# A conv-attention network's first pair: ones products on TensorE, a convolution shared by four engines, work made ahead; squares on ScalarE in layer 1; the last product in pieces

## The chip, the cores and the metric

The kernel runs on one core of one Trainium2 chip. The metric is device time in microseconds (us); lower is better. Times before are from three runs. Engines are named as in the profile: PE is TensorE, DVE is VectorE, ACT is ScalarE, POOL is GpSimd; SP only issues transfers here.

## What is computed

The input x is (2, 512, 32, 32) in float32; four layers follow one another. All arithmetic is float32.

```
layer 0: xn = bn(x);  q = grouped 1x1 conv of xn (8 groups of 64 channels)
         off = tanh(pw @ gelu(depthwise conv 6x6, stride 4, of q)) * 4      # 8x8 points per group
         kv  = bilinear samples of xn at the 64 shifted points;  k, v = grouped 1x1 convs of kv
         pos = query grid - shifted points;  bias = sign(pos) * log1p(|pos|)
         bias = w3 @ relu(w2 @ relu(w1 @ bias + b1) + b2) + b3               # 128 wide, 1024 x 64 positions
         x  += out_w @ softmax(q k / 8 + bias) v;   x += mlp(bn(x))
layer 1: linear attention: q, k of 64 channels brought to unit length, x += gamma * (v sums) / (n + q . sum k)
layer 2, 3: group norm, 8-head attention over 1024 positions, projection, residual
```

The bias network in layer 0 is evaluated for 2 x 8 groups, 64 sample points and 1024 queries; its second layer (w2) is the largest part of the kernel.

## The kernel before

**Layer 0** works through eight pairs of groups (a pair is 128 channels, pairs[0] to pairs[7]) and, for each group u, 16 steps of four sample points (`quads`: u, o, jj). For a step, `first_hidden` has DVE make the first hidden layer h1 (L528, four instructions of 1024 columns, each the sum of a row table x and a column table y, clipped at zero); `second_hidden` multiplies it on PE (L559, four q blocks of eight products; every product is two instructions), ScalarE takes the relu out of PSUM (L564), and ScalarE, GpSimd and adding transfers join the four blocks (flips of sign by ScalarE, L566 and L570, or by GpSimd, L568 and L575, both 128x1024). `last_product` adds into the logits, `attend` does the softmax. Two generators run behind this stream, one step at a time: `offsets` (from xn to the offsets and the logs of a pair) and `sampled` (samples, keys and values).

For pair 0, all of `offsets` runs before the stream begins. In it: xn (L295) on DVE, the padded query image qpad from products L308 and copies L317, the 36 taps of the strided convolution (for pair 0, 18 by ScalarE, L326, and 18 by DVE, L335, then two reductions over taps, L352), Gelu, the pw product (L368), Tanh, and from it the log of positions. Between steps 4 and 5 DVE prepares the last weights (`last_weights`, `fold_weights`). The tables x and y of pair 0's first points are made by masks (L492) and a product with a tile of ones, `self.all` (L499), read by L508 and L509. `sampled` transposes xn on PE (L413) and copies it by ScalarE (L414).

The order on PE, ACT, DVE and POOL is the order of the program text (`manual_schedule`); each engine takes its instructions in that order. PSUM holds a pool of three tiles of two banks (`ps`, shared by hp, transposes, tables and queries), one bank `self.bank` and one for the logits. Transfers are queued on SP (x, logs, results), on ACT (weights, at the start) and on POOL (the adding ones).

**Layer 1** has the order: products of queries and keys (L897) with additions on DVE (L900) for the two images and halves, squares on GpSimd (L908) after the second half of each image, `unit_length(0)` (L912 to L918), then 16 blocks of transposes (L927), copied to xT in turn by ACT and DVE (L930). The transposes use two PSUM pools of three tiles in turn; the products L897 use the second of them too. The products of keys with xT (L958) come later; they have 128x128 weights and 65 columns. Within the part whose order is written out GpSimd is not included.

**The end.** Layer 3's projection is seven products of half-size blocks per image (`project`); the last, P4, fills a PSUM tile with two blocks (p = 0, 1), then DVE adds each to x (L1489) and SP sends it out (L1497).

Of the kernel before, what the change touches and what calls it, by code (L numbers as in the profile page):

```python
# [18 lines left out]
P = 128  # L19
# [35 lines left out]
class Net:  # L55
# [16 lines left out]
    def prologue(self, ctx: ExitStack):  # L72
# [4 lines left out]
        nc.scalar.dma_start(self.cols, io["cols"])  # L77
# [21 lines left out]
    def layer0(self):  # L99
# [3 lines left out]
        with ExitStack() as ctx:  # L103
            keep = self.pool(ctx, "l0")
            self.l0qkv = keep.tile([P, 3, CT, P], F32, tag="qkv", name="qkv")
            nc.scalar.dma_start(self.l0qkv[:, 0], io["l0_qkv"][:, 0])
# [6 lines left out]
            last_weights = self.last_weights(keep)  # L113
            next(last_weights)
            nc.scalar.dma_start(self.l0qkv[:, 1:3], io["l0_qkv"][:, 1:3])
            ow = keep.tile([P, CT, C], F32, tag="ow", name="ow")
# [23 lines left out]
            with self.tc.manual_schedule(engines=engines):  # L140
                pairs = [{} for _ in range(BP)]
                for n, _ in enumerate(self.offsets(pairs[0], 0, ps)):
                    if n == 4:
                        nc.vector.tensor_copy(self.ys, self.grid[:, G_Y : G_Y + NB])
                        next(last_weights, None)
                        self.fold_weights()
                front = [self.sampled(pairs[0], 0, ps)]
                after, sims, att = [], {}, None
                tables = {}
                quads = [(u, o, jj) for u in range(2 * BP) for o in range(8) for jj in range(2)]  # L150
                ready = self.first_hidden(*quads[0], pairs, tables)
                held, self.join = [], None
                for i, (u, o, jj) in enumerate(quads):
# [12 lines left out]
                    else:  # L166
                        first = z
                        if len(held) == 2:
                            v, last, zs = held.pop(0)
                            self.last_product(v, last, zs, sims, ps_s)  # L170
                            if last == 7:
                                if v % 8 == 0:
                                    self.advance(after, lambda: False)
                                    att = [
                                        apool.tile([P, N], F32, tag=f"att{t}", name=f"att{v}_{t}") for t in range(CT)
                                    ]
# [44 lines left out]
    def last_weights(self, keep):  # L221
# [16 lines left out]
        nc.vector.tensor_tensor(self.flip, sign[:, 0:3], sign[:, 3:4].to_broadcast([P, 3]), ALU.mult)  # L238
        self.ends = keep.tile([P, 60], F32, tag="ends", name="ends")
        nc.vector.memset(self.ends, 0.0)  # L240
        for k in range(4):
            rows = slice(32 * k, 32 * k + 32)
            nc.vector.tensor_copy(self.ends[rows, 28 + k : 29 + k], sign[rows, 3:4])

# [43 lines left out]
    def offsets(self, m, bt, ps):  # L288
# [5 lines left out]
        xn = m["xn"] = self.fone.tile([P, N], F32, tag="xn", name=f"xn{b}{t}")  # L294
        nc.vector.tensor_scalar(xn, self.xs[b][t], self.s1[:, t : t + 1], self.col("bn1_b", t), ALU.mult, ALU.add)  # L295
        qp = m["q"] = self.fpool.tile([P, HP, HP], F32, tag="qpad", name=f"qpad{b}{t}")
        for edge in (qp[:, 0, :], qp[:, HP - 1, :], qp[:, :, 0], qp[:, :, HP - 1]):
            nc.gpsimd.memset(edge, 0.0)
        yield
        q = ps.tile([P, 2, HF], F32, tag="ps", name=f"q{b}{t}")  # L300
        qs = [q[:, par, :] for par in range(2)]
        if bt == 0:

            qs[1] = ps.tile([P, HF], F32, tag="ps", name="q001")
        for par in range(2):
            rows = slice(par * DH, (par + 1) * DH)
            for h in range(2):
                nc.tensor.matmul(  # L308
                    qs[par][h * DH : (h + 1) * DH, :],
                    lhsT=self.l0qkv[rows, 0, t, rows],  # L310
                    rhs=xn[rows, h * HF : (h + 1) * HF],
                    start=True,
                    stop=True,
                )
        for par in range(2):
            for h in range(2):
                (nc.scalar.copy if (par if bt == 0 else h == par) else nc.vector.tensor_copy)(  # L317
                    qp[par * DH : (par + 1) * DH, 1 + 16 * h : 17 + 16 * h, 1 : 1 + W],
                    qs[par][h * DH : (h + 1) * DH, :].rearrange("p (r w) -> p r w", w=W),
                )  # L320
        yield
        prod = self.fone.tile([P, 6, 6, NJ], F32, tag="prod", name=f"prod{b}{t}")
        own = 3 if bt == 0 else 6
        for ky in range(own, 6):
            for kx in range(6):
                nc.scalar.activation(  # L326
                    prod[:, ky, kx, :].rearrange("p (y x) -> p y x", y=8),
                    bass.AP(
                        tensor=qp.tensor, offset=qp[:, ky, kx : kx + 1].offset, ap=[list(qp.ap[0]), [4 * HP, 8], [4, 8]]
                    ),  # L330
                    AF.Copy,
                    scale=self.col("dw_w", 6 * ky + kx),
                )
        for ky in range(own):
            nc.vector.tensor_tensor(  # L335
                prod[:, ky, :, :].rearrange("p k (y x) -> p k y x", y=8),
                bass.AP(
                    tensor=qp.tensor,
                    offset=qp[:, ky, 0:1].offset,
                    ap=[list(qp.ap[0]), [1, 6], [4 * HP, 8], [4, 8]],  # L340
                ),
                self.taps[:, 6 * ky : 6 * ky + 6].unsqueeze(2).unsqueeze(3).to_broadcast([P, 6, 8, 8]),
                ALU.mult,
            )
            if ky % 2:
                yield
        conv = self.fpool.tile([P, NJ], F32, tag="conv", name=f"conv{b}{t}")
        if bt == 0:

            more = self.fpool.tile([P, NJ], F32, tag="ge", name="conv_more")  # L350
            for to, rows in ((conv, slice(0, 3)), (more, slice(3, 6))):
                nc.vector.tensor_reduce(to, prod[:, rows].rearrange("p a b j -> p j (a b)"), AX.X, ALU.add)  # L352
            nc.vector.tensor_tensor(conv, conv, more, ALU.add)
            yield
        else:
            for third in (slice(0, 24), slice(24, 44), slice(44, NJ)):
                nc.vector.tensor_reduce(
                    conv[:, third], prod[:, :, :, third].rearrange("p a b j -> p j (a b)"), AX.X, ALU.add
                )
                yield  # L360
        ge = self.fpool.tile([P, NJ], F32, tag="ge", name=f"ge{b}{t}")
        nc.scalar.activation(ge, conv, AF.Gelu, bias=self.col("dw_b"))
        yield
# [20 lines left out]
        yield  # L384
        log = self.fpool.tile([P, 2, W], F32, tag="log", name=f"log{b}{t}")
# [14 lines left out]

    def sampled(self, m, bt, ps):
# [5 lines left out]
        xn = m["xn"]  # L407
        spots = self.fone.tile([P, 2 * NJ, 2], F32, tag="spots", name=f"at{b}{t}")
        nc.sync.dma_start(spots, m["spots"].rearrange("k d -> (k d)").partition_broadcast(P))
        xnT = self.fone.tile([P, NB, P], F32, tag="xnT", name=f"xnT{b}{t}")  # L410
        tr = ps.tile([P, NB, P], F32, tag="ps", name=f"tr{b}{t}")
        for n in range(NB):
            nc.tensor.transpose(tr[:, n, :], xn[:, n * P : (n + 1) * P], self.ident)  # L413
        nc.scalar.copy(xnT, tr)  # L414
# [49 lines left out]
        yield  # L464

# [53 lines left out]
    def first_hidden(self, u, o, jj, pairs, tables):  # L519
# [4 lines left out]
        h1 = []  # L524
        for r in range(2):
            h = self.hid.tile([P, 2, H, W], F32, tag="h1", name=f"h1_{u}_{o}{jj}{r}")
            for k in range(2):
                self.nc.vector._custom_dve(  # L528
                    TENSOR_ADD_SAT,
                    out=h[:, k, :, :],  # L530
                    in0=x[:, jj, 2 * r + k, :].unsqueeze(1).to_broadcast([P, H, W]),
                    in1=y[:, jj, 2 * r + k, :].unsqueeze(2).to_broadcast([P, H, W]),
# [1262 lines left out]
```

## Time and profile before

| What | us |
|---|---|
| median of 3 runs (3364.01 to 3364.61) | 3364.38 |
| profiled execution, its own time | 3364.63 |
| its span | 3362.1 |
| PE busy | 3329.9 |
| PE busy, first 27 us | 4.4 |
| first L559 / steady L559 stream from | 27.0 / 40.54 |
| last PE instruction ends | 3357.7 |

Times inside the profile count from the span's start. Busy time of PE is modelled at its ends, since products overlap; where the pace matters, starts are compared. A wait is put down to what came last before the instruction.

### The profile page before, as it was taken

How to read it: one execution, taken by the hardware profiler on the slowest of the kernel's cores; microseconds unless marked ns; L12 is line 12 of the kernel's file. 1: busy time of each engine (PE TensorE's matmuls, PEld its weight loads, DVE VectorE, ACT ScalarE, POOL GpSimd, SP SyncE). 2: the span in 40 equal slices, each digit the busy share in tenths (PEclk: the TensorE clock that was granted, in tenths of full speed). 3: DMA queues.
4: the chain of work that ended last, by engine and by line, in shares of the span. 5: the costliest groups of instructions: out<-in, count | busy, mean ns of one | idle time of the engine just before them, and what ended most of it. 6: DMA issues, size and time to landing. Idle time of an engine off the chain costs nothing.

```text
span 3362.1 us, 60165 instructions
## 1 busy us (share of the span) xinstructions
PE 3329.9 (99%) x25224; PEld 1229.2 (37%) x25224; DVE 2316.6 (69%) x2519; ACT 2056.9 (61%) x2180; POOL 2171.8 (65%) x1649
## 2 busy tenths in 40 slices
PE   7999999999999999999999999999999999999999
PEld 2333333333333333333333334444465533455333
DVE  6776777777766676777776665565565678755787
ACT  6887887887887687887887771111121466213662
POOL 4877878877877677877878874333233447634475
PEclk9999999999999999999999999999999999999999
DMA  6777777877877577877878773111000100000001
GB/s 165 157 153 157 158 155 153 161 157 148 164 156 145 117 152 157 160 157 151 162 166 166 158 138 114 38 50 38 0 1 0 38 1 1 14 0 13 1 1 51
DMA packets 102383, 342.65 MB, mean 102 GB/s; under 512 B 12624, under 2 KB 14288, under 8 KB 99024
## 3 DMA queue, kind: packets, MB, share of 16 engines
q0 software_dynamic: 73296, 266.90, 40.7%
q1 hardware_dynamic: 27792, 69.68, 7.2%
q8 instruction: 203, 3.33, 0.4%
q10 hardware_dynamic: 1008, 2.06, 0.2%
q14 instruction: 84, 0.69, 0.1%
HBM read 67.27 MB, written 4.46 MB: 21 GB/s over the span
## 4 chain that ended last, share of the span: by engine, by line
PE 95%; DVE 2%; POOL 1%; ACT 1%; issue 1%; DMA 0%; ACTq 0%; POOLq 0%; DVEq 0%
PE hp L559 51%; PE s L1392 7%; PE o L1421 7%; PE sim L591 3%; PE qk30P L1170 1%; PE qk20P L1170 1%; PE m_6P L729 1%; PE m_4P L729 1%; PE m_3P L729 1%; PE m_1P L729 1%; PE m_0P L729 1%; PE qk31P L1170 1%; PE qk21P L1170 1%; PE m_5P L729 1%; PE m_2P L729 1%; PE m_7P L729 1%
## 5 line engine op out<-in xcount | busy, mean ns | idle before, releaser
L559 PE MATMUL hp<-h,w 128*32 128x512 f32 x16384 | 1799.4, 593 | 3.0 <-DVE h L528 2.0
L528 DVE CUSTOM_DVE_ANT_1 h<-tx,bank 128x1024 f32<-128x1024 f32 x1024 | 1180.7, 1216 | 309.1 <-PE hp L559 237.3
L564 ACT ACTIVATE h<-hp,magb 128x1024 f32<-128x1024 f32 x1024 | 1120.6, 1111 | 378.2 <-PE hp L559 372.8
L559 PEld LDWEIGHTS hp<-h,w 128*32 128x32 f32 x16384 | 526.3, 110 | 1205.9 <-issue 1150.7
L551 POOL DMA_DIRECT2D h<-h x509 | 451.6, 1022 | 384.7 <-ACT h L570 323.4
L577 POOL TENSOR_TENSOR h<-h,h 128x1024 f32<-128x1024 f32 x255 | 610.4, 2394 | 21.3
L575 POOL TENSOR_SCALAR h<-h,flip 128x1024 f32<-128x1024 f32 x256 | 447.1, 1746 | 0.9 <-ACT h L564 0.9
L1396 ACT ACTIVATE e<-s 128x1024 f32<-128x1024 f32 x256 | 261.8, 1024 | 155.5 <-PE s L1392 150.2
L566 ACT ACTIVATE h<-h,flip 128x1024 f32<-128x1024 f32 x256 | 291.3, 1138 | 0.0
L1392 PE MATMUL s<-q,k 64*64 64x512 f32 x2048 | 265.2, 589 | 0.0
L1421 PE MATMUL o<-e,v 64*64 64x512 f32 x2048 | 265.1, 589 | 0.0
L1403 POOL TENSOR_TENSOR some<-some,e 128x1024 f32<-128x1024 f32 x64 | 160.8, 2512 | 43.0 <-ACT e L1396 39.3
L1401 POOL TENSOR_TENSOR some<-e,e 128x1024 f32<-128x1024 f32 x32 | 75.7, 2366 | 157.4 <-DVE sum L1410 125.2
L568 POOL TENSOR_SCALAR h<-h,flip 128x1024 f32<-128x1024 f32 x128 | 143.0, 1117 | 52.0 <-ACT h L564 51.0
L570 ACT ACTIVATE h<-h,flip 128x1024 f32<-128x1024 f32 x128 | 145.7, 1138 | 0.0
L591 PE MATMUL sim<-h,ends 128*32 128x512 f32 x1024 | 135.2, 592 | 0.0
L1421 PEld LDWEIGHTS o<-e,v 64*64 64x64 f32 x2048 | 78.3, 133 | 141.4 <-issue 136.5
L1392 PEld LDWEIGHTS s<-q,k 64*64 64x64 f32 x2048 | 78.1, 133 | 141.0 <-issue 115.5
L1406 DVE TENSOR_TENSOR sum<-e,e 128x1024 f32<-128x1024 f32 x32 | 56.8, 1774 | 100.6 <-ACT e L1396 100.6
L707 POOL TENSOR_TENSOR mlp_w<-mlp_w 128x512 f32<-128x512 f32 x16 | 22.6, 1414 | 159.6 <-DMA mlp_w<-in_mlp_w 121.7
L788 ACT ACTIVATE mh<-mh,cols 128x512 f32<-128x512 f32 x64 | 46.2, 722 | 124.2 <-DVE mh L806 65.2
L1444 DVE RECIPROCAL r<-r 128x512 f32<-128x512 f32 x32 | 107.3, 3353 | 1.1
(527 smaller groups left out, 3294.0 us busy)
## 6 DMA issues: line engine op xcount, KB each, us to landing
h<-h POOLq DMA_DIRECT2D x509, 512.0 KB, 6.4
lb<-logs SPq DMA_DIRECT2D x63, 512.0 KB, 5.2
mlp_w<-in_mlp_w SPq DMA_DIRECT2D x16, 1024.0 KB, 4.8
x<-in_x SPq DMA_DIRECT2D x8, 512.0 KB, 9.7
qkw<-in_l_qk SPq DMA_DIRECT2D x2, 2048.0 KB, 7.5
out<-x SPq DMA_DIRECT2D x16, 256.0 KB, 2.1
vw<-in_l_v SPq DMA_DIRECT2D x2, 1024.0 KB, 7.7
projw<-in_l_proj SPq DMA_DIRECT2D x2, 1024.0 KB, 4.6
```

The source lines that it names most:

```text
L528: self.nc.vector._custom_dve(TENSOR_ADD_SAT, out=h[:, k, :, :], in0=x[:, jj, 2 * r + k, :].unsqueeze(1).to_broadcast([P, H, W]), in1=y[:, ...
L551: nc.gpsimd.dma_start(to, what, accum_op=ALU.add)
L559: nc.tensor.matmul(hp[rows, cut], lhsT=self.l0w2[:, 32 * q : 32 * q + 32], rhs=h1[k][:, cut], start=True, stop=True)
L564: nc.scalar.activation(y, hp, AF.Relu, bias=self.magb[:, q : q + 1])
L566: nc.scalar.activation(ys[0], ys[0], AF.Copy, scale=self.flip[:, 0:1])
L575: nc.gpsimd.tensor_scalar(y, y, self.flip[:, 2:3], 1.0, ALU.mult, ALU.mult)
L577: (nc.vector if final else nc.gpsimd).tensor_tensor(y, y, ys[2], ALU.add)
L591: nc.tensor.matmul(sims[u][at : at + 32, :], lhsT=self.ends[:, 28 - 4 * o : 60 - 4 * o], rhs=z[jj][:, h * HF : (h + 1) * HF], start=(o == ...
L729: self.nc.tensor.matmul(acc[p], lhsT=w[:, a, k, p * P : (p + 1) * P], rhs=right(r, k), start=k == 0, stop=k == 1)
L1392: nc.tensor.matmul(s[halves[c], par, :], lhsT=ks[p][rows, at : at + DH], rhs=qs[p][rows, cut], start=True, stop=True)
L1396: nc.scalar.activation(e, s, AF.Exp, scale=DH**-0.5)
L1421: nc.tensor.matmul(o[halves[par], r, :], lhsT=v[n // 2][rows, n % 2, at : at + DH], rhs=e[rows, par, :], start=(n == 0), stop=(n == NB - 1),)
```

## The change

Four things are changed. (1) Loads at the start: the query weights of pair 0 alone go first, then cols; the other pairs' query weights later. (2) Pair 0: TensorE multiplies ones by ones at three places; the convolution's 36 taps are split into 12 on DVE, 8 on ScalarE and 16 on TensorE, the last as products with diagonal matrices that GpSimd makes; the transposes of pairs 0, 1, 2 and the query products of pair 1 are made before the stream, kept in tiles that are not in use yet; the last weights' preparation is split (magb, sign and flip after Gelu; the folded weights, ends and ys after the positions); the very first h1 is made in halves of rows. (3) Layer 1's squares move from GpSimd to ScalarE. In the diff `queries` holds what `offsets` had of qpad's edges, products L308 and copies L317, and `turn` the transposes L413. (4) The last product of the kernel is done as one block of 512 columns and two of 256, in three PSUM tiles, each added and sent by itself.

```
-        nc.scalar.dma_start(self.cols, io["cols"])
...
-            nc.scalar.dma_start(self.l0qkv[:, 0], io["l0_qkv"][:, 0])
+            nc.scalar.dma_start(self.l0qkv[:, 0, 0], io["l0_qkv"][:, 0, 0])
+            nc.scalar.dma_start(self.cols, io["cols"])
...
             nc.scalar.dma_start(self.l0qkv[:, 1:3], io["l0_qkv"][:, 1:3])
+            nc.scalar.dma_start(self.l0qkv[:, 0, 1:CT], io["l0_qkv"][:, 0, 1:CT])
...
+                ones_ps = ps_s.tile([P, HF], F32, tag="sim", name="ones_ps")
+                def warm(n):
+                    for _ in range(n):
+                        nc.tensor.matmul(ones_ps[:, 0:P], lhsT=self.all, rhs=self.all, start=True, stop=True)
+                warm(13)
                 for n, _ in enumerate(self.offsets(pairs[0], 0, ps)):
-                    if n == 4:
-                        nc.vector.tensor_copy(self.ys, self.grid[:, G_Y : G_Y + NB])
-                        next(last_weights, None)
-                        self.fold_weights()
+                    if n == 1:
+                        warm(5)
+                    elif n == 2:
+                        first_tr = self.turn(pairs[0], 0, ps)
+                    elif n == 4:
+                        warm(11)
+                for t in (1, 2):
+                    self.normed(pairs[t], t, True)
+                pairs[0]["xT"] = self.fone.tile([P, NB, P], F32, tag="xnT", name="xnT00")
+                nc.scalar.copy(pairs[0]["xT"], first_tr)
                 front = [self.sampled(pairs[0], 0, ps)]
...
                 ready = self.first_hidden(*quads[0], pairs, tables)
+                att = [apool.tile([P, N], F32, tag=f"att{t}", name=f"att0_{t}") for t in range(CT)]
+                for t in (1, 2):
+                    tr = self.turn(pairs[t], t, ps)
+                    pairs[t]["xT"] = att[t].rearrange("p (n c) -> p n c", c=P)
+                    nc.scalar.copy(pairs[t]["xT"], tr)
+                    if t == 1:
+                        self.queries(pairs[1], 1, ps)
+                del pairs[2]["xn"]
...
     def offsets(self, m, bt, ps):
...
+        if "q" not in m:
+            self.normed(m, bt)
+            yield
+            self.queries(m, bt, ps)
+            yield
...
+        if bt == 0:
+            yield from self.first_conv(qp, prod, conv, ps)
+        else:
...
         nc.scalar.activation(ge, conv, AF.Gelu, bias=self.col("dw_b"))
+        if bt == 0:
+            next(self.weights)
         yield
...
+        if bt == 0:
+            self.fold_weights()
+            next(self.weights)
...
+    def first_conv(self, qp, prod, conv, ps):
+        nc, own, both = self.nc, 12, 20
+        diag = []
+        for k in range(both, len(TAPS)):
+            i = (k - both) % 8
+            if i == 0:
+                diag.append(self.hid2.tile([P, 8, P], F32, tag="h23", bufs=5, name=f"diag{k}"))
+            nc.gpsimd.tensor_scalar(diag[-1][:, i, :], self.ident, self.col("dw_w", k), 1.0, ALU.mult, ALU.mult)
+        acc = ps.tile([P, NJ], F32, tag="ps", name="conv_ps")
+        for k in range(both, len(TAPS)):
+            nc.tensor.matmul(
+                acc.rearrange("p (y x) -> p y x", y=8),
+                lhsT=diag[(k - both) // 8][:, (k - both) % 8, :],
+                rhs=self.window(qp, k),
+                start=(k == both),
+                stop=(k == len(TAPS) - 1),
+            )
+        for k in range(own, both):
+            nc.scalar.activation(
+                prod[:, k // 6, k % 6, :].rearrange("p (y x) -> p y x", y=8),
+                self.window(qp, k),
+                AF.Copy,
+                scale=self.col("dw_w", k),
+            )
+        for k in range(0, own, 6):
+            nc.vector.tensor_tensor(
+                prod[:, k // 6, :, :].rearrange("p k (y x) -> p k y x", y=8),
+                self.window(qp, k, 6),
+                self.taps[:, k : k + 6].unsqueeze(2).unsqueeze(3).to_broadcast([P, 6, 8, 8]),
+                ALU.mult,
+            )
+        more = self.bank[:, 0:NJ]
+        for to, cut in ((conv, slice(0, own)), (more, slice(own, both))):
+            nc.vector.tensor_reduce(to, prod.rearrange("p a b j -> p j (a b)")[:, :, cut], AX.X, ALU.add)
+        nc.vector.tensor_tensor(conv, conv, more, ALU.add)
+        nc.vector.tensor_tensor(conv, conv, acc, ALU.add)
+        yield
...
+    def normed(self, m, bt, ahead=False):
+        nc = self.nc
+        b, t = divmod(bt, CT)
+        if ahead:
+            xn = self.hid2.tile([P, N], F32, tag="h23", bufs=5, name=f"xn{b}{t}")
+        else:
+            xn = self.fone.tile([P, N], F32, tag="xn", name=f"xn{b}{t}")
+        m["xn"] = xn
+        (nc.gpsimd if ahead else nc.vector).tensor_scalar(
+            xn, self.xs[b][t], self.s1[:, t : t + 1], self.col("bn1_b", t), ALU.mult, ALU.add
+        )
+
+    def queries(self, m, bt, ps):
...
...
-                (nc.scalar.copy if (par if bt == 0 else h == par) else nc.vector.tensor_copy)(
+                (nc.scalar.copy if bt == 1 or (par if bt == 0 else h == par) else nc.vector.tensor_copy)(
...
     def sampled(self, m, bt, ps):
+        if "xT" not in m:
+            xT = self.fone.tile([P, NB, P], F32, tag="xnT", name=f"xnT{b}{t}")
+            nc.scalar.copy(xT, self.turn(m, bt, ps))
+            m["xT"] = xT
...
+    def turn(self, m, bt, ps):
+        tr = ps.tile([P, NB, P], F32, tag="ps", name=f"tr{bt}")
+        for n in range(NB):
+            self.nc.tensor.transpose(tr[:, n, :], m["xn"][:, n * P : (n + 1) * P], self.ident)
+        return tr
...
     def first_hidden(self, u, o, jj, pairs, tables):
+        parts = 2 if (u, o, jj) == (0, 0, 0) else 1
+        for c in range(parts):
+            cut = slice(c * H // parts, (c + 1) * H // parts)
+            for r in range(2):
+                for k in range(2):
+                    self.nc.vector._custom_dve(
+                        TENSOR_ADD_SAT,
+                        out=h1[r][:, k, cut, :],
+                        in0=x[:, jj, 2 * r + k, :].unsqueeze(1).to_broadcast([P, H // parts, W]),
+                        in1=y[:, jj, 2 * r + k, cut].unsqueeze(2).to_broadcast([P, H // parts, W]),
+                        s0=F32_MAX,
+                        s1=0.0,
+                    )
...
-                    nc.gpsimd.tensor_tensor(sqs[b], qk[b], qk[b], ALU.mult)
+                    nc.scalar.activation(sqs[b], qk[b], AF.Square)
...
+                    if out is not None and b == 1 and which == "P4":
+                        for p, lo, hi, spot in ((0, 0, HF, None), (1, 0, HF // 2, "odd"), (1, HF // 2, HF, "even")):
+                            piece = acc[:, 0, :] if spot is None else place(spot, f"pb{k}{lo}")[:, 0, lo:hi]
+                            for c in range(2):
+                                nc.tensor.matmul(piece, lhsT=left[a][:, c, p * P : (p + 1) * P],
+                                    rhs=right[b][ri][c][:, lo:hi], start=c == 0, stop=c == 1)
+                            xt = self.xs[b][2 + p][:, lo:hi]
+                            vec.scalar_tensor_tensor(xt, piece, self.col(f"pb{k}", 2 + p), xt, ALU.add, ALU.add)
+                            nc.sync.dma_start(out[b, 2 + p][:, lo:hi], xt)
+                        yield
+                        continue
```

## The prediction

> **What bounds the kernel now.** I read the page's first part, then busy time by stretches, then the chain that ended last in its first 41 us, and last the waits and the chain at the two later places that the change touches.
>
> ```profile
> PE 3329.9 (99%) x25224; PEld 1229.2 (37%) x25224; DVE 2316.6 (69%) x2519; ACT 2056.9 (61%) x2180; POOL 2171.8 (65%) x1649
> ```
>
> ```profile
> 0.00:27.00 27.00, 4.41 (x16) 1.83 (x17) 14.38 (x33) 12.62 (x31) 1.19 (x11) 1.00 0.62 233
> 27.00:41.00 14.00, 13.48 (x81) 5.46 (x85) 8.94 (x10) 7.68 (x8) 3.03 (x3) 1.00 0.45 107
> ...
> 100.00:2020.00 1920.00, 1919.25 (x17648) 591.46 (x17640) 1380.54 (x1382) 1534.25 (x1526) 1503.85 (x1209) 1.00 0.77 154
> ```
>
> The stretches read: busy us of PE, weight load, DVE, ScalarE, GpSimd, each with its instructions. PE is the bound: after 41 us it is never free for long (1919.25 of 1920 us in the long stretch). Its 32 idle us are mostly the first 27, where it worked 4.4. So only two things can shorten this kernel: reaching the steady stream of products earlier, and taking work out of the stream. The chain of the start, times from the span's start:
>
> ```profile
> 1.17 5.88 DMA qkv<-in_l_qkv
> ...
> 10.76 5.48 ACT prod L326 x18
> ...
> 16.27 2.09 DVE conv_more L352
> ...
> 22.92 2.06 PE lb_ps L499 x4
> ...
> 27.00 7.36 PE hp L559 x35
> ...
> 37.58 2.01 ACT h L564 x2
> 39.59 0.91 ACT xnT L414
> ```
>
> (Columns: start, length, engine, tile, line.) A chain of load, query product at 7.18, convolution, small DVE work, table, h1; then one second-hidden group that starts thinly (27.0), ends at 37.8, and a wait for ScalarE until 40.54, where PE begins to stream. The start is also at a slow clock: same line, same shape,
>
> ```profile
> L559 PE MATMUL hp<-h,w x37: 592/593/1062, 27.0 to 33.8; 128*32 128x512 f32 x37
> ```
>
> the 1062 are those before about 31 us, the 592 all later ones. In the stream four such instructions lie side by side and a set takes 0.43 us.
>
> **The start, step by step** (new time against old).
> *Loads.* The first slab of query weights (64 KB) goes ahead of cols (70 KB). cols landed at 4.97 and the 256 KB behind it 2.1 us later, about 0.5 us per 64 KB; so cols lands near 5.6 (bounds 5.0 and 7.05, where the second transfer landed before). xn follows as before 1.2 us later: q at 6.8 against 7.18.
> *Products of ones.* 13 products are 26 instructions of 128 columns. The cold L499 instructions have 256 columns at 0.43 apiece, so these cost 0.21, 5.5 us, from 1.1 (the ones are set at 0.88 + 0.20) to 6.6: no delay of q. They cost nothing while they end before q; each us over costs one.
> *The clock, rule against row.* The row: the clock rose about 4.2 us after the first L559 product. [...] By the row the clock is up at 5.3; [...] and in the bad case q stays cold, +0.9. [...] I take the row; 0.9 goes into the range.
> *q* at full clock: two sets of four, 2 x 0.43 + 0.2 = 1.05, ends 7.85 (9.17). The copies into qpad take 1.4 as before: 9.3 (10.7).
> *Convolution.* Before, 18 taps on ScalarE (5.48) and two reductions in a row. Now DVE has 12 taps: 2 x 0.77 to 10.9, reduction 12/18 of 2.10 = 1.40 to 12.3, that of ScalarE's 8 taps (8 x 0.304, ready 11.8) 8/18 of 2.08 = 0.92 to 13.2, two adds of 0.23 to 13.7. PE has 16 taps, 32 instructions with 128x128 weights and 64 columns; the nearest row is L958, 64 of 65 columns in 7.31, 0.114 each: 3.65, to 13.0, ahead of DVE's last add. GpSimd builds 16 diagonals of 128x128 from 5.7 on. No row has this; the nearest is its select that makes ident, same tile, 0.288: 4.6, to 10.3, the first eight by 8.0. Per element L568 (1117 ns for 1024) would give 0.14 each, and if an instruction were dear whatever its size 1.117. I take 0.29 and keep 1.117. ge at 13.75 (18.64).
> *Small work.* Before, tanh's result was ready at 19.64 and DVE took it at 20.71, behind the last-weight preparation. Split in two, that hides under ge and under Abs/Ln/Sign (DVE waited 0.76 there). Then ScalarE is late: tanh, table load 1.28, the early Ln 0.20, which comes 0.2 before the old time of Abs. So ge to the log product 3.25 (3.44): 17.0 (22.08). The transposes of pair 0 (1.09) stand on PE between convolution and the pw product: 13.0 to 14.1, and ge ends at 14.1; free, but any later convolution pays here. The 11 products of ones (22 x 0.11 = 2.4) end at 16.9, before the table product.
> *Table and h1.* The masks take 0.84: L499 at 17.85 (22.92), 1.3 at full clock (2.06; the later L499 pairs ran so), y 0.5: h1 at 19.75 (25.64). ScalarE's new copy of pair 0's transposes (1.02, behind g) ends at 18.2, before x is due at 18.55. In halves h1 costs eight times about 0.61 (half of 1.14 plus 0.04), 4.9: whole at 24.65 (30.2). Only one of eight product groups can use the first halves.
> *First group.* 14 sets of 0.43 from 24.7: last result 30.9 (37.8). ScalarE then sets the resumption: relu at 25.7 and 27.4, then steps of 1.04 for two flips and two relus, done at 32.7. Pair 0's transposes and copy no longer stand behind them, so the next group gets its PSUM tile at 32.7 (40.54). **Start: -7.8.**
>
> **Work moved out of the stream.** Pair 1's and 2's transposes (8 x 0.109 = 0.87 each) and pair 1's query products (two sets, 0.86) now run from 19.2 to about 22, while PE waits for h1. ScalarE copies them (1.02 twice, 4 x 0.58), done by 24.1, before the first relu. In the full stream each is worth its length: **-2.6.** If this cover ended late, it would delay the first group one for one. Pair 2's second xn (0.81 on DVE) hides at 69%. xn for pairs 1, 2 goes behind the diagonals on GpSimd, 2 x 1.75, to about 14; nobody waits before 19.
>
> **Layer 1's squares.**
>
> ```profile
> DVE r L912 <- POOL sq L908: 0.8, 1, 0.8
> ...
> PE l1t L927 <- DVE qk L900: 0.9, 1, 0.9
> ```
>
> With ScalarE idle, the first squares (L566's shape, 1.14) are ready early; DVE's 0.8 goes, and the fourth qk addition ends at 2446.4 instead of 2447.2. But ScalarE takes its work in order: the second squares stand ahead of the copies of xT and wait for that addition, 2446.45 to 2447.55. The copy of transposed block 0, which began at 2444.89, ends at 2448.1, and block 6 needs its PSUM tile; PE reaches it at 2446.9. PE then loses 0.2 + 1.25 instead of 1.0 (start to start): **+0.4.** Bounds: -0.8 if no copy is late. [...] every load in this trace is 1.283. If Square needs a switch here, +1.7 by the row [...]. Identity and Abs came without loads, Square is as simple; I take +0.4.
>
> **The last product in pieces.**
>
> ```profile
> 3357.71 0.06 DVE x L1489
> ...
> 3358.38 0.74 DVE x L1489
> ```
>
> Both final additions waited for all eight instructions and end at 3359.12; the output transfer ends the span at 3362.1. In pieces the first (0.74) runs from 3356.9, behind DVE's adds for the product before; then two of 256 columns (0.4, steps 0.35), the last from about 3357.95 to 3358.3. One more issue on SP, 0.35 to 0.4 apiece, keeps pace. **-0.85** (-0.5 to -1.1).
>
> **Sum.** -7.8 - 2.6 + 0.4 - 0.85 = -10.85 from the profiled execution's 3364.63 (span 3362.1 and 2.5 around it), 3353.8; the median shown is 0.25 below that execution, so 3353.5 to 3353.8. I forecast 3353.8, its own range 3351 to 3357.
>
> **Rivals.** 0.2%, 6.7 us, is about what a measurement here tells from no change.
> *A, the loads or a small step come late* (chance 0.14): cols at 7.05, q cold, or DVE's chain 1 us longer each shift everything behind: 1.5 to 3 us, about 3356. For it: ten short steps that I add without slack. Against: each has a row.
> *B, moved work isn't repaid* (0.07): PE would wait where it worked, 3356.4. Against it the 0.75 idle us in 1920.
> *C, the change doesn't keep the clock up* (0.06). q +0.9; convolution at 0.22, 7 us, to 17.3; cold transposes to 19.05; 11 cold products of ones to 24.2; table to 26.3; moved work cold, 5.2, to 31.5. The first group then gains nothing but the missing pair-0 work: about 1 us at the start, 3360.5. The 4 us of the row speak against it.
> *D, slower: the diagonals* (0.03). PE's convolution ends 1.8 after the last diagonal, and it may end at 13.4; from 0.37 us per diagonal on, every us delays all. The saving is gone at (11.6 + 10.85 - 5.7) / 16 = 1.05 us each. At L568's whole 1.117 it is 3366; at L575's mean 1.746 for the same operation, 16 of them end at 33.6 and the kernel takes about 3375.8.
>
> Forecast 0.70. A, B and the forecast are all faster by over 0.2% but for their tails (0.04); C is within it, D counts as slower. So faster 0.87, within 0.10, slower 0.03. Range 3350.5 to 3359: below, a Square without late copies and cheaper steps; above, A together with a table switch.
>
> **What would show it.** Right: L559 without 1062 ns forms, first one near 22.5 and streaming from about 33; 16 GpSimd instructions near 0.3; ge near 13.8; PE idle under 14 us in the first 33; in layer 1 a PE wait for ScalarE's copy of about 1.3. Wrong: a PE wait on GpSimd for a diagonal, a table load at the squares, PE idle in the long stretch by us rather than tenths, or q's set at 1.07 us per instruction.

## The result, and the profile after

The changed kernel takes 3351.05 us (median of 6 runs, 3350.72 to 3351.23) against 3364.49 of the kernel before (6 runs): a ratio of 0.9959, 95% interval 0.9949 to 0.9969. The forecast was 3353.8. The span of the profiled execution is 3349.3 us (before 3362.1); 1.85 us lie outside it (before 2.5, and so in all runs of either kernel; why is open).

First the page's row of busy time, then the stretches (busy us of PE, weight load, DVE, ScalarE, GpSimd with counts; granted clock, DMA share, GB/s):

```profile
PE 3336.1 (100%) x25318; PEld 1242.6 (37%) x25318; DVE 2310.4 (69%) x2521; ACT 2056.0 (61%) x2173; POOL 2176.0 (65%) x1665
```

```profile
0.00:27.00 27.00, 23.66 (x166) 18.43 (x170) 17.37 (x41) 15.12 (x29) 9.93 (x33) 1.00 0.76 250
27.00:41.00 14.00, 13.47 (x118) 5.63 (x114) 10.27 (x12) 10.84 (x12) 7.39 (x7) 1.00 0.37 93
```

PE is still the bound, and busy 23.66 of the first 27 us instead of 4.4; 9.5 of these are the products of ones. The chain that ended last, from the logs to the steady stream (start, length, engine, tile, line):

```profile
18.07 0.24 DVE log L382
...
18.90 1.10 PE lb_ps L586 x4
20.00 0.87 PE tr L550 x8
20.87 1.02 PE q L469 x8
21.89 1.02 PE tr L550 x8
22.92 5.46 PE hp L649 x35
...
31.59 2.02 ACT h L654 x2
33.61 0.04 issue
33.66 7.48 PE hp L649 x65
```

The stream begins at 33.66 (before 40.54), and its products are at full clock from the first one:

```profile
L649 PE MATMUL hp<-h,w x16384: 589/592/618, 22.8 to 1997.8; 128*32 128x512 f32 x200
```

Aligning the two traces by the starts of the same instructions gives the account. All are us of span, after minus before:

| Where | forecast | measured |
|---|---|---|
| start, to the steady stream | -7.8 | -6.9 |
| steady stream of layer 0 | -2.6 | -5.9 |
| end of layer 0 | 0 | +0.6 |
| layer 1's squares | +0.4 | -1.07 |
| end of the kernel | -0.85 | +0.4 |
| sum | -10.85 | -12.9 |

Two terms have the wrong sign, one is more than twice its size, and one stood in no sum. The experiments take the terms in turn, but for the end of layer 0; each is compared with the changed kernel's 3351.05. They were measured in several sessions, in which the kernel before had medians of 3364.44 to 3364.84; so differences under about 0.4 us are read from the traces, not from the times.

### The profile page after: what moved, and what is told of

The parts are those of the page before. It is cut to its first block, busy times and chain, and to the rows that moved or that the text cites. A ratio compares the mean times of both kernels' runs of the same rounds, so it can differ in the third digit from the quotient of the medians.

```text
span 3349.3 us, 60380 instructions
## 1 busy us (share of the span) xinstructions
PE 3336.1 (100%) x25318; PEld 1242.6 (37%) x25318; DVE 2310.4 (69%) x2521; ACT 2056.0 (61%) x2173; POOL 2176.0 (65%) x1665
## 4 chain that ended last, share of the span: by engine, by line
PE 96%; DVE 1%; POOL 1%; issue 1%; DMA 0%; ACT 0%; ACTq 0%; POOLq 0%; DVEq 0%
PE hp L649 51%; PE s L1482 7%; PE o L1511 7%; PE sim L681 3%; PE qk30P L1260 1%; PE qk20P L1260 1%; PE qk31P L1260 1%; PE m_6P L819 1%; PE m_5P L819 1%; PE m_3P L819 1%; PE m_1P L819 1%; PE m_0P L819 1%; PE qk21P L1260 1%; PE m_7P L819 1%; PE m_4P L819 1%; PE m_2P L819 1%
## 5 line engine op out<-in xcount | busy, mean ns | idle before, releaser
L618 DVE CUSTOM_DVE_ANT_1 h<-tx,bank 128x1024 f32<-128x1024 f32 (+1 forms) x1028 | 1181.0, 1212 | 310.2 <-PE hp L649 239.1
```

The lines of the kernel that those rows point to most:

```text
L618: self.nc.vector._custom_dve(TENSOR_ADD_SAT, out=h1[r][:, k, cut, :], in0=x[:, jj, 2 * r + k, :].unsqueeze(1).to_broadcast([P, H // parts, ...
```

## Experiments

**The products of ones.** Left out altogether; nothing of the result depends on them.

```diff
-                warm(13)
...
-                    if n == 1:
-                        warm(5)
-                    elif n == 2:
+                    if n == 2:
                         first_tr = self.turn(pairs[0], 0, ps)
-                    elif n == 4:
-                        warm(11)
```

> The changed kernel (3351.05 us) without its 29 products of ones. My theory: the ones bring the clock up before the query product; without them that product is at half clock (+0.9), and the convolution on PE runs at half clock for about 4 us of work before the clock rises (ends near 16.8 instead of 14.0), so that Gelu and everything behind it come 2.5 to 4 us later: 3353.5 to 3355. Rival: the clock stays at half until the first L649 group, as in the kernel before: +6.5, 3357.5. Rival: the convolution on PE alone warms it in time and nothing is lost: 3351.

3356.63 us, 5.6 slower. PE's timeline at the start (start, length, line, operation, shapes, count; idle time before it and what ended that):

```profile
11.04 7.06 PE L403 MATMUL conv_ps<-qpad,diag 128*128 128x64 f32 x32 [1.57 <-DVE qpad L467]
17.91 1.88 PE L539 MATMUL tr<-ident,xn 128*128 128x128 f32 x8
19.72 0.28 PE L346 MATMUL bank<-cols,ge 64*64 64x2 f32 x4
23.19 2.05 PE L575 MATMUL lb_ps<-first,all 128*128 128x256 f32 x4 [3.19 <-DVE first L568]
...
38.89 1.49 PE L638 MATMUL hp<-h,w 128*32 128x512 f32 x12 [0.31 <-ACT h L643]
```

For comparison, two lines of the changed kernel:

```profile
10.24 3.97 PE L414 MATMUL conv_ps<-qpad,diag 128*128 128x64 f32 x32 [0.26 <-POOL diag L411]
...
15.63 2.72 PE L149 MATMUL ones_ps<-all 128*128 128x128 f32 x22
```

Without the ones the whole convolution ran at half clock, 7.06 us instead of 3.97, and DVE's last addition waited 2.7 us for it. The trace's record of the granted clock rises only at 19.64, 8.6 us after the convolution began, falls at 23.05 behind the idle 3.19 us, and rises again at 26.46: steps of 3.41 us in this trace. My 4 us were too short for this. Why the clock did not rise earlier under the convolution's products of 64 columns, 6.9 us of them from 11.04, is open; each takes as long there (0.21 us from start to start) as the transposes behind it, which have 128. The rise comes 1.7 us after the first of those transposes (17.91); whether they had a part in it was not tested.

**The convolution.** The old split (18 taps on DVE, 18 on ScalarE, none on PE), with all else as changed.

```diff
-        nc, own, both = self.nc, 12, 20
+        nc, own = self.nc, 18
...
-            nc.gpsimd.tensor_scalar(diag[-1][:, i, :], self.ident, self.col("dw_w", k), 1.0, ALU.mult, ALU.mult)
...
-        for k in range(own, both):
+        for k in range(own, len(TAPS)):
...
```

> The changed kernel with pair 0's convolution as before: 18 taps on DVE, 18 on ScalarE, no diagonals and no products for it. If the clock stays up, Gelu comes 3.0 us later (ScalarE's taps end at 15.7, second reduction and add at 18.05, against 15.02): 3354.1. My theory: PE then idles 7 us between the transposes and the pw product, the clock falls, the 11 products of ones run at half rate (4.7 us) and end about 1.5 us after the table product could start, which itself takes 0.75 more: +5 to 5.5, 3356 to 3356.6. Rival: the convolution's share is hidden by the loads or the diagonals anyway: +1 or less.

3356.46 us, 5.4 slower (its twelve runs spread from 3355.10 to 3357.93; the one in the trace took 3355.47): ge comes at 17.87 instead of 15.02, and that delay is not all:

```profile
9.57 1.04 PE L534 MATMUL tr<-ident,xn 128*128 128x128 f32 x8
18.27 0.38 PE L357 MATMUL bank<-cols,ge 64*64 64x2 f32 x4 [7.66 <-ACT ge L349]
18.58 4.88 PE L149 MATMUL ones_ps<-all 128*128 128x128 f32 x22
23.30 1.03 PE L570 MATMUL lb_ps<-first,all 128*128 128x256 f32 x4
```

PE is idle for 7.66 us, the clock falls to half from 12.9 to 23.15, and the last ones take 4.88 us instead of 2.72, past the time the table product could start. The convolution on PE is also the work that carries the clock from the first ones to the second. So the gains of ones and convolution do not add: taking out either costs over 5 us, of the 6.9 that the start gained in all.

**The order of the first loads.** cols ahead of the first query weights.

```diff
-            nc.scalar.dma_start(self.l0qkv[:, 0, 0], io["l0_qkv"][:, 0, 0])
             nc.scalar.dma_start(self.cols, io["cols"])
+            nc.scalar.dma_start(self.l0qkv[:, 0, 0], io["l0_qkv"][:, 0, 0])
```

> The changed kernel with cols again ahead of pair 0's query weights on ScalarE's queue (both stay small transfers). My theory: putting cols second cost 1.5 us of its landing (6.50 against 4.97), which xn, the diagonals and the query product waited for, and the slab behind it would land in time; with cols first xn ends near 6.0 and q starts when the 13 products of ones end, near 6.6 instead of 7.58: -0.8 to -1.0, 3350.1. Rival: the slab is then what q waits for, as before the change (7.18): -0.4, 3350.65. The prediction's step (cols behind a 64 KB transfer lands 0.6 later only) would make this -0.3 at most.

3350.53 us, 0.5 faster. cols lands at 5.16 instead of 6.50, but now q waits for its weights and starts at 6.80 (7.58):

```profile
6.80 1.09 PE L469 MATMUL q<-xn,qkv 64*64 64x512 f32 x8 [0.63 <-DMA qkv<-in_l_qkv]
```

The stream begins at 33.05, against 33.66 in the changed kernel's trace and 33.37 to 33.46 in those of e2, e3, e4 and e10, which load in the changed kernel's order.

**Work moved out of the stream.** Two runs put parts back: pair 1's queries (with its xn, and the copies into qpad shared with DVE as before), and all of pair 2's xn and transposes.

```diff
-                    if t == 1:
-                        self.queries(pairs[1], 1, ps)
-                del pairs[2]["xn"]
+                del pairs[1]["xn"], pairs[2]["xn"]
...
```

> The changed kernel with pair 1's xn and query products back in the stream of products, its transposes still ahead. The prediction's step: +0.86, 3351.9. My theory: +1.17 (the products 1.02 and two broken sets of L649, 0.15) and +2.4, since pair 1's offsets get their two steps back as in the run with two empty steps: 3354.5.

```diff
-                for t in (1, 2):
+                for t in (1,):
                     self.normed(pairs[t], t, True)
...
-                for t in (1, 2):
+                for t in (1,):
                     tr = self.turn(pairs[t], t, ps)
...
```

> The changed kernel with pair 2's transposes back in the stream (its xn made once, by DVE). The prediction's step: +0.87, 3351.9. My theory from the two traces: the stream loses the 1.02 us of the transposes and 0.14 in the sets around them, +1.16: 3352.2. Rival: nothing, the time being lost elsewhere: 3351.05.

3354.48 us (+3.4) and 3352.60 us (+1.55). A group of eight takes 1.02 us of the stream, not the 0.87 of its own pace (here the transposes in e7):

```profile
425.61 1.09 PE L549 MATMUL tr<-ident,xn 128*128 128x128 f32 x8
426.63 4.93 PE L648 MATMUL hp<-h,w 128*32 128x512 f32 x44
```

The four-fold sets lose some 0.14 us around it. By the starts of the same products it is 1.16 each in e6 and e7, 3.5 for the three. The transposes' extra 0.4 us are not in e7's trace, whose run was the fastest of five (3352.05); they are not accounted for. The queries cost three times their length, and the reason is not the queries. Before the change ScalarE ran this in the middle of the stream:

```profile
192.48 1.11 ACT L564 ACTIVATE h<-hp,magb 128x1024 f32<-128x1024 f32 x1
193.60 1.28 ACT L626 ACT_TABLE_LOAD   x1
194.90 0.63 ACT L626 ACTIVATE e<-e 128x512 f32<-128x512 f32 x1
195.44 0.24 ACT L386 ACTIVATE log<-pos 128x64 f32<-128x64 f32 x1
195.69 1.28 ACT L387 ACT_TABLE_LOAD   x1
196.99 0.26 ACT L387 ACTIVATE log<-log 128x64 f32<-128x64 f32 x1
```

and in the changed kernel at the same step:

```profile
182.80 1.11 ACT L654 ACTIVATE h<-hp,magb 128x1024 f32<-128x1024 f32 x1
183.92 1.28 ACT L716 ACT_TABLE_LOAD   x1
185.22 0.63 ACT L716 ACTIVATE e<-e 128x512 f32<-128x512 f32 x1
185.75 2.10 ACT L654 ACTIVATE h<-hp,magb 128x1024 f32<-128x1024 f32 x2
```

Pair 1's logs used to fall between the first softmax's Exp and the next relu, with a table load of their own: 3.7 us without a relu, and PE ran dry:

```profile
198.44 1.07 PE L559 MATMUL hp<-h,w 128*32 128x512 f32 x8 [0.65 <-ACT h L564]
```

With its queries made ahead, pair 1's generator has two steps less, so its logs come before the softmax. The test leaves the queries where the change put them and only adds two empty steps:

```diff
             self.queries(m, bt, ps)
             yield
+        elif bt == 1:
+            yield
+            yield
```

> The changed kernel with two empty steps at the head of pair 1's offsets, which leaves all work as it is and puts pair 1's later steps back where they stood before. My theory: the stream gained 2.45 us beyond the moved work because pair 1's logs no longer come between the first softmax's Exp and the relus of the same step, with a table load each way; with the two steps back the stalls return: +2.4, 3353.5. Rival: the 2.45 come from somewhere else (pair 1's copies, the transfers that start earlier): no change, 3351.05.

3353.60 us, 2.55 slower, with no instruction of the program added; by the starts of the same products the stream is 2.5 longer. The table load of the logs is back, and PE's wait for the relu with it (first ScalarE's timeline, then PE's):

```profile
185.29 1.28 ACT L719 ACT_TABLE_LOAD   x1
...
187.38 1.28 ACT L382 ACT_TABLE_LOAD   x1
```

```profile
190.13 8.79 PE L652 MATMUL hp<-h,w 128*32 128x512 f32 x80 [0.65 <-ACT h L657]
```

**Layer 1's squares** back on GpSimd.

```diff
-                    nc.scalar.activation(sqs[b], qk[b], AF.Square)
+                    nc.gpsimd.tensor_tensor(sqs[b], qk[b], qk[b], ALU.mult)
```

> The changed kernel with layer 1's squares back on GpSimd. My theory, from the two traces: PE's wait of 0.9 us at the transposes comes back, since DVE waits for the squares and the table load for Sqrt waits for DVE again: +1.07, 3352.1. Rival, the prediction's step (squares on ScalarE make the copies of xT late): the change cost 0.4 here and undoing it gives 3350.6.

3352.50 us, 1.45 slower; PE's wait of 0.89 us at the transposes is back, and the trace is 1.1 longer at this place (first PE in e2, then in the changed kernel, which does not wait):

```profile
2434.81 1.42 PE L1017 MATMUL l1t<-ident,x 128*128 128x128 f32 x11 [0.89 <-DVE qk L990]
```

```profile
2431.88 5.29 PE L1017 MATMUL l1t<-ident,x 128*128 128x128 f32 x47
```

The reading is in the changed kernel's ScalarE timeline:

```profile
2425.65 1.06 ACT L998 ACTIVATE sq<-qk 128x1024 f32<-128x1024 f32 x1 [27.83 <-DVE qk L990]
2426.73 1.28 ACT L1003 ACT_TABLE_LOAD   x1
2430.35 0.21 ACT L1003 ACTIVATE r<-r 128x16 f32<-128x16 f32 x1 [2.34 <-DVE r L1002]
2432.81 1.06 ACT L998 ACTIVATE sq<-qk 128x1024 f32<-128x1024 f32 x1 [2.25 <-DVE qk L990]
2433.78 0.57 ACT L1020 COPY xT<-l1t 128x512 f32<-128x512 f32 x1
```

Square has no load of its own here, and the Sqrt's load now runs directly behind it, 3.6 us before the Sqrt itself, which waits for DVE's sum of squares. With the squares on GpSimd, Sqrt is ScalarE's first instruction since 2397 and has several things to wait for, in wait instructions of their own; the load stands behind these (here e2, and so before):

```profile
2431.03 1.28 ACT L1003 ACT_TABLE_LOAD   x1 [33.50 <-DVE r L1002]
2432.32 0.22 ACT L1003 ACTIVATE r<-r 128x16 f32<-128x16 f32 x1
```

Its 1.28 us then stood in DVE's way. In the changed kernel Square has taken over these waits, and the one that is left sits in the Sqrt instruction, behind the load. e2 brings two delays of DVE back at once, 1.3 us for the load and 0.85 for the squares themselves; no run parts them.

**The end of the kernel.** First the old end (one tile, two output transfers) with all else as changed.

```diff
-                    if out is not None and b == 1 and which == "P4":
+                    if False:
```

> The changed kernel with the last product as one block of both rows again. The prediction's step says +0.85: 3351.9. My theory from the traces: the two transfers of 1 KB rows are issued slower (0.58 and 0.41 us against 0.33) and land later (2.5 to 2.9 against 2.0 to 2.1), which eats the 0.8 that DVE gains, and SP has more semaphores to read after the last landing: undoing it gives the same or up to 0.45 less, 3350.6 to 3351.05.

3350.89 us: no slower than with the pieces (0.16 less). The pieces do let DVE end 0.8 us earlier, but their transfers are slower. Two lines on the last transfers of the changed kernel (issue times min/median/max in ns; then us from issue to landing):

```profile
L1608 SPq DMA_DIRECT2D out<-x x3: 332/405/584, 3344.3 to 3345.4; - x3
...
DMA to landing us min/median/max: 2.5/2.8/2.9
```

I took the rows for the cause, 1 KB against 2 KB, and found a second oddity: before the kernel ends, SP waits on semaphores, the counters that tell of landed transfers, in twelve reads one after another, 0.06 us apiece. In the kernel before, the last transfer's came last; the additional transfers of the change turn the numbers round, so that it comes early and six or seven reads still follow its landing. Three runs separate these: two pieces of 512 columns in tiles of their own; the old end with one transfer less (the other query weights in a single load); and both together with cols first.

```diff
-                        for p, lo, hi, spot in ((0, 0, HF, None), (1, 0, HF // 2, "odd"), (1, HF // 2, HF, "even")):
+                        for p, lo, hi, spot in ((0, 0, HF, None), (1, 0, HF, "odd")):
```

> The last product as two pieces of 512 columns, each in its own PSUM tile, loads as in the changed kernel. Theory: the size of the rows sets the price of the last transfers, so the landing comes about 0.65 us earlier than with pieces of 256 columns, while the order of SP's last reads costs what it costs in the changed kernel or less: about 3350.4 us. Rival: pieces make no difference, as e3 with one tile and 3350.9 us against 3351.05 seemed to say: 3350.9 to 3351.0 us.

```diff
-            nc.scalar.dma_start(self.l0qkv[:, 1:3], io["l0_qkv"][:, 1:3])
-            nc.scalar.dma_start(self.l0qkv[:, 0, 1:CT], io["l0_qkv"][:, 0, 1:CT])
+            rest = "p a t c -> p (a t c)"
+            nc.scalar.dma_start(self.l0qkv.rearrange(rest)[:, P:], io["l0_qkv"].rearrange(rest)[:, P:])
...
```

> The old end of the kernel (one tile for the last product, as e3) and the rest of the query weights in one transfer instead of two, so that there are as many transfers in all as in the kernel before. Theory: the last output transfer has the last number of SP's reads again, and the span ends about 0.06 us after it has landed instead of 0.49 us: 0.45 us less than e3, about 3350.45 us. Rival: the reads run on whatever the number, or the one larger transfer lands later and delays the queries of pair 1: 3350.9 us, e3's time, or more.

> Three edits to the changed kernel at once: cols loaded ahead of the first query weights (as e5), the last product as two pieces of 512 columns instead of one of 512 and two of 256, and the rest of the query weights in one transfer instead of two. Theory: the start gains 0.5 us (what e5 measured); the tail keeps rows of 2 KB, so the two output transfers take 0.33 us apiece to issue and land 2.1 us later, about 0.65 us earlier than in the changed kernel; and with one transfer less at the start and one less at the end the numbers of the last semaphores are those of the kernel before, so that SP reads the last one last: 0.45 us less. In all 3349.5 us. Rival, that the last landing comes at 7.1 us after the last product's first instruction whatever the pieces, and that the order of reading is no cost: 3350.5 us, e5's time.

3350.80 (e10), 3351.24 (e11) and 3350.73 us (e9): none of my three totals. The traces tell why. From the end of the last product to the end of the span, us:

| | pieces | last transfer's semaphore is read | us |
|---|---|---|---|
| before | one tile | last | 4.47 |
| changed | 512 + 256 + 256 | early | 4.83 |
| e3 | one tile | early | 4.89 |
| e10 | 512 + 512 | early | 4.87 |
| e11 | one tile | last | 4.48 |
| e9 | 512 + 512 | last | 4.45 |

The order of the reads is worth 0.41 us (e3 to e11, e10 to e9); pieces are worth nothing at any size. In the other runs with the changed kernel's end (e1, e2, e4 to e8) this time is 4.76 to 5.39. So the length of the rows is not the cause: e9's transfers of 2 KB rows also take 2.5 to 2.7 us to land. Its DMA activity from 3346.10 to 3347.55 (last issue at 3345.30, landing at 3347.98), tenths of 16 engines in 40 slices:

```profile
DMA  1929495985969598794545000001001010101000
...
q14 instruction: 1, 0.01, 1.3%
```

and the same stretch of e3 (last issue at 3345.59, landing 2.03 us later):

```profile
DMA  9798696959599495977959597795632000000000
```

In e9 the data are through in 0.8 us, but for one engine that still sends for 0.5 us more; an instruction fetch of 8 KB, 0.31 us on one engine, lies in this stretch. In the changed kernel, e9 and e10 a fetch starts 0.8 to 0.9 us behind the last issue and the last transfer lands after 2.5 to 2.7 us; in the kernel before, e3, e11 and e12 it starts 0.4 us ahead of that issue and the landing takes 2.05. The other seven traces lie along the same line: 2.10 us with a fetch 0.3 ahead (e1), 2.3 to 2.5 with one 0.0 to 0.4 behind (e4, e5, e7, e8), 2.7 to 2.9 with one 1.0 behind (e2, e6). That the fetch holds up the engine is how I read this; no run moved the fetch alone.

In e9 and e11 the start lost what the end gained: steady products from 33.76 and 33.99, instead of the 33.05 of e5 and the 33.41 of e3. DVE and GpSimd in e9:

```profile
14.88 0.16 DVE L264 TENSOR_TENSOR flip<-sign 128x3 f32<-128x3 f32 x1
15.26 0.97 DVE L364 SCALAR_TENSOR_TENSOR at<-at,grid 128x2 f32<-128x2 f32 x1 [0.21 <-ACT at L359]
```

```profile
15.03 1.19 POOL L450 TENSOR_SCALAR xn<-x,bn1s,cols 128x1024 f32<-128x1024 f32 x1 [2.49 <-DMA x<-in_x]
```

A DVE instruction over two columns takes 0.97 us instead of 0.16 and ends together with GpSimd's xn. In both runs x of pair 2 came late behind the single load, and GpSimd's xn for it fell upon DVE's short chain; in e11 it is another instruction of the same kind, L258, from 14.73 to 15.70. In the changed kernel GpSimd is through just as that chain begins.

The last run takes the same number of transfers without touching the loads: cols first, the old end, and one block of the first image's result sent in one transfer.

```diff
+                    if (b, p, i) == (0, 0, 2):
+                        cut = slice(0, N)
-                    if out is not None:
+                    if out is not None and (b, p, i) != (0, 0, 3):
                         nc.sync.dma_start(out[b, o][:, cut], self.xs[b][o][:, cut])
...
```

> Three edits to the changed kernel: cols ahead of the first query weights (as e5), the old end with one tile for the last product (as e3), and one transfer less, this time by sending one 1024-column block of the first image's result as one transfer instead of two, which leaves the loads of the start alone. Theory from the runs before: e5's 3350.53 us, less 0.16 (e3's end for the new one), less 0.41 (the reads after the last landing, as from e3 to e11): 3350.0 us, with steady products from 33.05 us, since x of pair 2 is not delayed and GpSimd's second xn is over before VectorE's small instructions begin, and with 4.48 us from the last product's end to the span's end. Rival: that the 0.7 to 0.8 us which e9 and e11 lost in the start have another cause than the single load of the query weights, or that the larger transfer delays the end: 3350.5 to 3351 us.

3350.02 us (3349.93 to 3350.15; ratio to the kernel before 0.9955, 0.9941 to 0.9969): the fastest of all, with the stream from 33.07, as expected. This kernel does without the change's fourth part.

## Why the prediction was right, and where not

The total lies in the range and on the right side, but that it lies so near is in part luck: without their signs the misses of the table's five terms sum to 7.5 us, with them to 2.0.

*Loads* failed: cols at 6.50, not 5.6, and q at 7.58, not 6.8. A 64 KB load ahead of it made cols 1.34 us later than in e5 (5.16), not 0.5 to 0.6. e5 shows the order to be wrong by 0.5 us.

*Products of ones*, *the clock* and *q* held: the clock is up at 5.81, 4.7 us after the first ones, and q takes 1.09 us (1.05). The row's 4.2 us is no constant, though: with the same ones the clock came 4.0 (e5) to 6.2 us (e11) after the first, at 5.09 to 7.32. In e11 q followed only 0.1 us later; that q was never cold is in part luck. That this clock has to be carried on over the convolution was not in the sum; rival C, priced at 6.7 us, is what the kernel without ones shows but for the size (5.6, e1).

*Convolution*: 16 diagonals take 6.04 us, 0.378 each instead of 0.29 (fifteen take 0.37, and one that starts while DVE makes xn takes 0.84), just at the 0.37 from which rival D begins to cost; PE waits for them only 0.26 us. The two reductions take 1.53 and 1.07 (1.40, 0.92). ge comes at 15.02 instead of 13.75, of which 0.8 is q's. *Small work* was right (3.05, forecast 3.25), *table and h1* a little better (1.10 for the product, 1.3): h1 at 20.67, forecast 19.75. *First group*: 33.66, forecast 32.7, the delay of h1 passed on.

*Work moved out of the stream* failed by what it left out. I priced the lengths of three groups (2.6; with the breaks 3.5) and did not follow that the generator behind the stream has fewer steps. The other 2.4 us are a table load that no longer falls between a softmax and a relu (e4: 2.55). The profile before had it: PE's wait of 0.65 us at 197.8 hides in the 0.75 idle us that I took for nothing, and sets spread wider than 0.43 us don't show as idle at all.

*Layer 1's squares* has the wrong sign. The late copies of xT were to cost 1.25 us; the step missed is the place of the Sqrt's table load, which leaves the path of DVE. DVE's fourth addition comes 0.9 us after the first transpose, where I had 2.4; the second square ends at 2433.87, the first copy at 2434.35, and PE needs that tile at about 2434.5 (24 transposes of 0.109 after 2431.88). A switch at Square, with which this term would have been +1.7, did not come: no load stands before the Squares at 2425.65 and 2432.81. (The switch shown above at 193.60 took 1.3 us from the end of one function to the start of the next.)

*The last product in pieces* failed: the time to the last add was right (0.8), but the landing and the order of the reads weren't in the sum. The +0.4 is the order of the reads.

*End of layer 0*, +0.6, was in no term: PE waits 0.34 and 1.79 us for DVE's softmax of the last group (before 0.71, with about 1 us lost earlier in L591):

```profile
2016.32 0.66 PE L725 MATMUL bank<-ident,e 128*128 128x128 f32 x4 [1.79 <-DVE e L721]
```

All runs show these waits, the longer one with 1.7 to 1.8 us but for e8's 1.2; I did not test what sets them.

Rivals A and B: A happened in part (0.9 us); B did not.

## What to carry to other kernels

Taking steps out of a generator that runs behind a stream brings all its later instructions forward: look where its table loads and its waits land, for that was worth 2.4 us here, beside 3.5 for the work removed. Where the products begin at half clock, as here, keep TensorE busy until the stream begins (5.6 us here, e1), and count each piece of real work between as part of this cover (the convolution's, 5.4 us, e8). At the end, count to the last landing (2.0 to 2.9 us behind its issue here) and to the last read behind it (0.41 us), not to the last computation.

## What the runs showed of the hardware

- A ScalarE table load stood behind the separate wait instructions of its function (e2: 33.5 us idle, then the load), but ahead of the one wait which the function carries itself (changed kernel: the load 3.6 us before its Sqrt). Square, without a load of its own and with the other waits taken first, put the load's 1.28 us under the last wait.
- A small DVE scalar_tensor_tensor started during a GpSimd tensor_scalar of 128x1024 ended only with it: 0.97 us instead of 0.16 (e9, e11). Two-tensor additions in the same situation took their usual 0.22 (14.44 us in the changed kernel, beside GpSimd's xn from 12.60 to 14.96), but one of their two inputs was in PSUM (`bank`, `conv_ps`), where both of the slow ones' were in SBUF; which difference counts was not tested.
- From half rate, the clock rose 4.0 to 6.2 us after the first of dense products of 128 columns (twelve traces), and 8.6 us after the first of the convolution's products of 64 columns (e1).
- SP's closing reads cost 0.06 us each; one transfer less in the program, at its start (e11) or before its end (e12), put the last landing's read last again, worth 0.41 us.
